# A list schedule in which an exponential of a two-head tile waits for both heads' row maxima

## The chip, the core and the metric

The kernel runs on one core of one Trainium2 chip. A core has five engines with an instruction queue each, which are worked off in order: PE (matmuls; its weight loads are shown as PEld), DVE, ACT, POOL and SP, which here issues the DMAs. The metric is the device time of one execution in microseconds. Times quoted as "the profile's" are from one profiled execution, counted from its first instruction.

## What is computed

One transformer layer with post-normalisation, in float32, over 2 sequences of 1024 tokens of 512 features: causal attention with 16 heads of 32 features, then a feed-forward part whose weights are reduced to their signs.

```python
qkv = x @ w_qkv.T + b_qkv                       # 1536 columns: q, k, v of 16 heads of 32
scores = q @ k.T / sqrt(32) + causal mask       # 1024 x 1024 for each head and sequence
attn = softmax(scores) @ v
x = layernorm(x + attn @ w_out.T + b_out)
hidden = relu((x @ sign(up).T) * up_scale)      # 2048 columns
y = (hidden @ sign(down).T) * down_scale * output_scale
return layernorm(x + y)
```

## The kernel before

**A planner orders everything.** The kernel doesn't write its instructions out in the order in which they run. It describes tasks: which engines can do each (a copy out of PSUM may go to DVE or ACT), what it reads and writes, how long it keeps the engine and when its result is there, and a `place`, which is its priority. `Plan.schedule()` is a list scheduler over these: it steps through a modelled time, gives each free engine the ripe task with the smallest place, and has each buffer class hand out its buffers in the order of places. The order found is recorded under `tc.manual_schedule()`, and each engine's queue follows it. The semaphore waits between engines are put in afterwards, from what the recorded instructions read and write; they are not the planner's. So an edge that the planner does not know changes only the order: the chip still waits as its semaphores say.

**Attention** runs over 8 chunks (2 sequences by 4 groups of four heads). In each chunk come 8 query tiles of 128 rows, i = 0 to 7; tile i sees (i+1)x128 keys. `grouped` says how many heads share one buffer of scores: four for i = 0 and 1, two for i = 2 and 3, one from i = 4 on. In the first chunk it is two heads for i = 0 to 3. So there are 36 tiles of two heads (the profile has 36 L902 on 128x2), with 72 of the 256 exponentials. The last chunk takes its tiles in the order 0, 1, 2, 7, 6, 5, 4, 3.

A tile of scores goes through these steps; the numbers are lines of the kernel:
- L837 on PE writes the scores into one of two PSUM buffers `d` (class "sc", two banks each); L818 does so in the first half of the first chunk, from 32-row operands.
- With one or two heads, L875 on DVE adds the mask and takes the negated row maximum, one instruction per head. With four heads L857 and L867 do it for all four at once.
- L890 on ACT takes the exponential of each head, with that maximum as bias, and sums the rows. When the last one is done the buffer `d` is free for the scores of the next tile but one.
- L902 on DVE takes the reciprocals of the sums, and L908 on POOL multiplies by them.
- L929 on PE transposes the probabilities, 128x128 at a time, four into one PSUM bank `s`; L491 (ACT) or L493 (DVE) copies each bank out.
- L958 on PE multiplies by the values, for all heads of a query tile, and L978 on DVE stores the result in `atT`.

**What fills PE between these steps** is the projection of the next chunk: L553 (keys and queries; their results leave by L632 and L637, or L574, L615 and L620) and L590 (values). In the last chunk it is the output of the second sequence (L1023 on PE; L1017 on POOL adds the bias to the row block `rows`, which has one buffer and comes by DMA; L1034 on DVE adds both), transposes of the first feed-forward block (L1091, copied out by L1098 on ACT and L1103 on DVE), and signs of the weights (L1117 on ACT, from `raw`, which a DMA of 1 MB fills). The feed-forward part (L1140 up, L1177 down) follows.

The scheduler's dependences of the exponential of head j, in `scores`: it reads parts `sc[1, j]`, which the mask or the maximum of head j writes, and `nm[j]`, the maximum itself. With four heads all parts are written by the one mask and the one maximum. With two heads, head 0's exponential is ripe in the planner as soon as head 0's maximum is done.

Of the kernel before, what the change touches and what calls it, by code (L numbers as in the profile page):

```python
# [276 lines left out]
def kernel(  # L277
# [169 lines left out]
    def of(t):  # L447
        if t.cls in rings:
            return rings[t.cls][0][:, t.slot * P : (t.slot + t.blocks) * P]
        if homes[t.cls][t.slot] is None:  # L450
            reopen(t.cls)
        return homes[t.cls][t.slot]
# [16 lines left out]
    def fp32(n):  # L469
        return {"PE": (n / 600 + 0.009,) * 2}  # L470
# [3 lines left out]
    def dve(us):  # L474
        return {"DVE": (us - 0.09, us)}

    def act(us):
        return {"ACT": (us - 0.09, us)}
# [23 lines left out]
    def new(cls, after=(), blocks=1):  # L502
        t = plan.tile(cls, [y for c in after for y in all_of[c]], blocks)
        all_of[cls].append(t)
        return t

    def dma(place, dst, src, kb, reads=(), writes=(), updates=(), queue=DMA, label="dma", after=()):
        def fn(e):
            engine[e].dma_start(dst(), src())

        return plan.task(
            queue, fn, place, reads, writes, updates, size=kb, label=label, after=after
        )
# [3 lines left out]
    def load_x(b, place, blocks):  # L517
        if b not in inputs:
            inputs[b] = new("xT")
        t = inputs[b]  # L520
        for t0 in blocks:
            for c in range(NC):
                latest["x"] = dma(
                    place,
                    lambda t=t, c=c, t0=t0: of(t)[:, c, t0 : t0 + TB],
                    lambda b=b, c=c, t0=t0: xT[ts(c, P), b * S + t0 : b * S + t0 + TB],
                    256,
                    updates=[t[c, t0]],
                )

    def load_w(b, e, place, parts, queue=DMA, after=()):
        if (b, e) not in weights:
            weights[b, e] = new("w")
        t = weights[b, e]
        for n in parts:
            dma(
                place,
                lambda t=t, n=n: of(t)[:, :, n, :],
                lambda n=n, e=e: w_qkvT[:, n * D + e * P : n * D + (e + 1) * P].rearrange(
                    "(c p) f -> p c f", p=P  # L540
                ),
                256,
                updates=[t[n]],
                queue=queue,
                after=after,
            )
# [19 lines left out]
    def bank(ps):  # L566
        return of(ps).rearrange("p a b -> p (a b)")
# [128 lines left out]
    def hold(src, parts, dst, held):  # L696

        for d, h in zip(dst, held):
            plan.task(
                dve(0.15), lambda _, d=d: nc.vector.tensor_copy(d(), src()), -200, parts, [h],  # L700
                label="hold",
            )

    def first_half():

        warm, busy = new("f"), a_x1[:, :P]
        nc.vector.memset(busy, 1.0)
        for k in range(WARM):
            plan.task(
                {"PE": (0.3, 0.3)},  # L710
                lambda _, k=k: nc.tensor.matmul(
                    of(warm)[:, k % 4, :], lhsT=busy, rhs=busy, start=True, stop=True
                ), -300, updates=[warm[0]], label="warm",
            )
        act_queue = {"ACT": (0.5, 0.5)}
        w, biases = new("w"), new("bqk")
        weights[0, 0] = w
        for c, z, n in ((0, 1, 1), (0, 1, 0), (1, NC, 1), (1, NC, 0)):
            dma(
                -100,  # L720
                lambda c=c, z=z, n=n: of(w)[:, c:z, n, :],
                lambda c=c, z=z, n=n: w_qkvT[c * P : z * P, n * D : n * D + P].rearrange(
                    "(c p) f -> p c f", p=P
                ),
                64 * (z - c),
                writes=[w[n, k] for k in range(c, z)],
                queue=act_queue,
            )
            if n == 0 and c == 0:
                dma(-100, lambda: bqk, lambda: b_qkvP, 8, writes=[biases[0]], queue=act_queue)  # L730
        xt = inputs[0] = new("xT")
        for c in range(NC):
            dma(
                -100,
                lambda c=c: of(xt)[:, c, :TB],
                lambda c=c: xT[ts(c, P), :TB],
                256,
                updates=[xt[c, 0]],
            )
        hold(  # L740
            lambda: of(xt)[:, 0, 0:1], [xt[0, 0]],
            [lambda: of(w)[:, 0, 2, 0:1], *[lambda c=c: of(xt)[:, c, TB : TB + 1] for c in range(NC)]],
            [w[2], *[xt[c, TB] for c in range(NC)]],
        )
        load_w(0, 0, -90, [2])
        load_x(0, -80, [TB])
        v, kq = new("v"), new("pt", blocks=8)
        rows = lambda n: of(kq)[:, n * TB : (n + 1) * TB]
        both = {n: new("f") for n in (1, 0)}
        for c in range(NC):  # L750
            for n in (1, 0):
                plan.task(
                    fp32(TB),
                    lambda _, c=c, n=n: nc.tensor.matmul(  # L754
                        bank(both[n]),
                        lhsT=of(w)[:, c, n, :],
                        rhs=of(xt)[:, c, :TB],
                        start=(c == 0),
                        stop=(c == NC - 1),
                    ),  # L760
                    -50, [xt[c, 0], w[n, c]], updates=[both[n][0]], count=2,
                    label="ps",
                )
        for n in (1, 0):
            bias = bqk[:, n * NC : n * NC + 1]
            if n == 0:
                plan.task(
                    dve(0.74),
                    lambda _, bias=bias: nc.vector.tensor_scalar(
                        rows(0), bank(both[0]), bias, scale, ALU.add, ALU.mult  # L770
                    ),
                    -50, [both[0][0], biases[0]], [kq[0]], label="bias",
                )
            else:
                plan.task(
                    act(0.69),
                    lambda _, bias=bias: nc.scalar.activation(
                        rows(1), bank(both[1]), AF.Identity, bias=bias
                    ),
                    -50, [both[1][0], biases[0]], [kq[1]], label="bias",  # L780
                )
        values_of(0, 0, v, 0, lambda units=0: -1)
        plain[0, 0] = kq, v
# [25 lines left out]
    def scores(b, e, i, heads, at):  # L809
        G, N, W = len(heads), (i + 1) * P, 2 * TB // len(heads)  # L810
        sc, nm, sums = new("sc"), new("nm"), new("sums")
        pr = new("pr", blocks=G * (i + 1))
        if (b, e) in plain and i < NQ // 2:
            kq = plain[b, e][0]

            def fn(_):
# [11 lines left out]
                updates=[sc[0]], count=2 * G, label="sc4",  # L828
            )
        else:  # L830
            st = made[b, e][0]
            for j, u in enumerate(heads):
                for k0 in range(0, N, TB):
                    k1 = min(k0 + TB, N)

                    def fn(_, j=j, u=u, k0=k0, k1=k1):
# [11 lines left out]
                        updates=[sc[0]], label="sc",  # L848
# [21 lines left out]
        else:  # L870
            for j in range(G):
# [3 lines left out]
                    lambda _, j=j, some=some: nc.vector.tensor_tensor_reduce(  # L875
                        some(),
                        some(),
                        mask[:, S - N :],
                        scale=-1.0,
                        scalar=LARGEST,  # L880
                        op0=ALU.add,
                        op1=ALU.min,
                        accum_out=of(nm)[:, j : j + 1],
# [3 lines left out]
        for j in range(G):  # L887
            plan.task(
                {"ACT": (0.25 + 0.852 * N / 1000, 0.37 + 0.852 * N / 1000)},
                lambda _, j=j: nc.scalar.activation(  # L890
                    of(pr)[:, j * N : (j + 1) * N],
                    of(sc)[:, j * W : j * W + N],
                    AF.Exp,
                    bias=of(nm)[:, j : j + 1],
                    scale=sign,
                    accum_out=of(sums)[:, j : j + 1],
                ),
                at, [sc[1, j], nm[j]], [pr[j], sums[0]], label="exp",
            )
        plan.task(  # L900
            dve(0.16),
# [3 lines left out]
        for j in range(G):  # L905
            plan.task(
                pool(0.254 + 0.843 * N / 1000),
                lambda _, j=j: nc.gpsimd.tensor_scalar(  # L908
                    of(pr)[:, j * N : (j + 1) * N],
                    of(pr)[:, j * N : (j + 1) * N],  # L910
                    of(sums)[:, j : j + 1],
                    1.0,
                    ALU.mult,
                    ALU.mult,
                ),
# [324 lines left out]


    first_half()
    second_half()
    for at, (b, e) in enumerate(chunks):
# [114 lines left out]
```

## Time and profile before

| what | value |
|---|---|
| time, median of 3 runs | 768.37 us (768.11 to 768.95) |
| the profiled execution | 768.15 us |
| its span, first to last instruction | 766.4 us |
| granted PE clock | 0.998 |
| PE busy | 753.0 us, 98% |
| DVE, ACT, POOL busy | 487.5, 374.9, 258.5 us |
| chain that ended last | PE 90%, DVE 6%, ACT 2%, DMA 1% |

"Busy" is the union of an engine's instruction records. A row of the timeline reads: start, length, engine, line, operation, output and input by name, shapes, count, and in brackets how long the engine was idle ahead of it and whose result ended that. A row of a windows answer gives the window, its length, and the busy time of each engine with its number of instructions. In all rows L numbers are lines of the kernel. DVE writes the maximum itself with a short extra record (DVE_READ_ACCUMULATOR2, 0.14 us), and ACT its row sum with another (ACTIVATION_READ_ACCUMULATOR, 0.2 us).

### The profile page before, as it was taken

To read this page: it belongs to the slowest core of one execution; us is meant where nothing else is said; L and a number is where in the kernel's file an instruction comes from. 1 tells how busy PE (TensorE), PEld (TensorE's weight loads), DVE (VectorE), ACT (ScalarE), POOL (GpSimd) and SP (SyncE) were. 2 spreads that over 40 slices of the span, in tenths; PEclk is the share of its full clock that TensorE was granted. 3 is DMA by queue.
4 is the path that set the end of the run, shared out by engine and by line. 5 is a ranking of instruction groups with operands and counts; after the bars stand their busy time and mean duration, and the time that the engine had idled before them with its cause. 6 is when DMAs were issued, how large, how long until landed. Compare 5 with 4: busy or idle time off the path is not lost.

```text
span 766.4 us, 15395 instructions
## 1 busy us (share of the span) xinstructions
PE 753.0 (98%) x5858; PEld 571.3 (75%) x5858; DVE 487.5 (64%) x1165; ACT 374.9 (49%) x831; POOL 258.5 (34%) x328
## 2 busy tenths in 40 slices
PE   9999999999999999999999999999999999999995
PEld 5668768769756766886876986658777887778884
DVE  2657777777856678877877778855336337335525
ACT  2458666765834465676676587733223222222210
POOL 2426445445525453544544545531002002002000
PEclk9999999999999999999999999999999999999999
DMA  6577345156354225514505523333001001000101
GB/s 189 125 161 152 106 99 125 41 111 170 107 125 102 65 69 110 110 46 91 132 1 113 124 75 122 137 110 110 0 1 56 0 1 56 0 1 1 55 1 55
DMA packets 38216, 62.35 MB, mean 81 GB/s; under 512 B 6144, under 2 KB 18432, under 8 KB 38144
## 3 DMA queue, kind: packets, MB, share of 16 engines
q1 hardware_dynamic: 36912, 60.85, 31.1%
q8 instruction: 46, 0.75, 0.4%
q10 hardware_dynamic: 1232, 0.53, 0.3%
q14 instruction: 26, 0.21, 0.1%
HBM read 24.66 MB, written 4.19 MB: 38 GB/s over the span
## 4 chain that ended last, share of the span: by engine, by line
PE 90%; DVE 6%; ACT 2%; DMA 1%; issue 1%; POOL 0%; ACTq 0%
PE s L929 15%; PE s L1140 14%; PE pd L1177 14%; PE s L553 12%; PE d L837 9%; PE s L958 8%; PE s L590 8%; PE s L1023 7%; DVE d L875 2%; ACT probs L890 1%; PE s L754 1%; PE s L1091 1%; DVE small L1207 1%; DMA rows<-in_x 1%; PE d L818 1%
## 5 line engine op out<-in xcount | busy, mean ns | idle before, releaser
L908 POOL TENSOR_SCALAR probs<-probs,small 128x128 f32<-128x128 f32 (+7 forms) x256 | 188.5, 747 | 235.7 <-DVE small L902 194.0
L890 ACT ACTIVATE probs<-d,small 128x128 f32<-128x128 f32 (+7 forms) x256 | 189.9, 750 | 50.8 <-DVE small L875 25.3
L875 DVE CUSTOM_DVE_ANT_0 d<-d,mask 128x384 f32<-128x384 f32 (+7 forms) x200 | 173.7, 876 | 25.3 <-PE d L837 20.2
L929 PE MATMUL s<-ident,probs 128*128 128x128 f32 x1152 | 160.1, 273 | 0.8 <-DVE small L902 0.4
L491 ACT COPY probsT<-s 128x512 f32<-128x512 f32 (+3 forms) x193 | 98.4, 542 | 127.1 <-PE s L929 113.3
L929 PEld LDWEIGHTS s<-ident,probs 128*128 128x128 f32 x1152 | 133.3, 141 | 32.2 <-issue 23.2
L1177 PE MATMUL pd<-stacks,hid 128*128 128x512 f32 x512 | 133.0, 399 | 0.5 <-DVE hid L1157 0.5
L1140 PE MATMUL s<-xt,stacks 128*128 128x512 f32 x512 | 132.7, 399 | 0.0
L1151 ACT ACTIVATE hf<-s,ups 128x512 f32<-128x512 f32 x64 | 44.1, 690 | 164.3 <-PE s L1140 162.5
L553 PE MATMUL s<-xT,wqkv 128*128 128x512 f32 x240 | 119.2, 597 | 0.0
L837 PE MATMUL d<-stacks 128*128 128x512 f32 (+2 forms) x368 | 114.0, 409 | 2.8 <-ACT probs L890 2.8
L1177 PEld LDWEIGHTS pd<-stacks,hid 128*128 128x128 f32 x512 | 94.1, 188 | 24.2 <-DVE hid L1157 1.4
L1140 PEld LDWEIGHTS s<-xt,stacks 128*128 128x128 f32 x512 | 94.2, 188 | 23.4 <-issue 1.0
L1157 DVE CAST hid<-hf 128x512 fp32r<-128x512 f32 x64 | 27.3, 427 | 121.6 <-ACT hf L1151 121.5
L493 DVE COPY probsT<-s 128x512 f32<-128x512 f32 (+3 forms) x152 | 83.7, 561 | 24.7 <-PE s L929 22.5
L837 PEld LDWEIGHTS d<-stacks 128*128 128x128 f32 x368 | 58.2, 189 | 38.5 <-ACT probs L890 19.6
L590 PE MATMUL s<-wqkv,xT 128*128 128x128 f32 x512 | 75.9, 275 | 0.0
L590 PEld LDWEIGHTS s<-wqkv,xT 128*128 128x128 f32 x512 | 68.6, 191 | 8.8 <-issue 7.3
L958 PEld LDWEIGHTS s<-probsT,v 128*32 128x32 f32 x2304 | 60.3, 110 | 19.3 <-ACT probs L890 7.6
L958 PE MATMUL s<-probsT,v 128*32 128x128 f32 x2304 | 71.7, 274 | 0.0
L1023 PE MATMUL s<-wout,atT 128*128 128x512 f32 x128 | 63.5, 596 | 0.4 <-ACT probsT L491 0.4
L890 ACT ACTIVATION_READ_ACCUMULATOR probs<-d,small 128x1 f32 x256 | 53.2, 208 | 0.0
(68 smaller groups left out, 492.4 us busy)
## 6 DMA issues: line engine op xcount, KB each, us to landing
stacks<-wqkv SPq DMA_DIRECT2D x224, 128.0 KB, 2.4
wqkv<-in_w_qkvT SPq DMA_DIRECT2D x22, 256.0 KB, 3.3
xT<-in_xT SPq DMA_DIRECT2D x16, 256.0 KB, 4.7
rows<-in_x SPq DMA_DIRECT2D x16, 256.0 KB, 2.8
raw<-in_up_wT SPq DMA_DIRECT2D x4, 1024.0 KB, 5.0
out<-atT SPq DMA_DIRECT2D x16, 256.0 KB, 2.0
stacks<-wqkv SPq DMA_DIRECT2D x48, 64.0 KB, 2.0
raw<-in_down_wT SPq DMA_DIRECT2D x2, 1024.0 KB, 5.4
```

The lines of the kernel that those rows point to most:

```text
L491: nc.scalar.copy(dst, src)
L553: nc.tensor.matmul(of(ps).rearrange("p a b -> p (a b)"), lhsT=of(w)[:, c, n, :], rhs=of(xt)[:, c, t0 : t0 + TB], start=(c == 0), stop=(c = ...
L590: nc.tensor.matmul(of(ps)[:, t, :], lhsT=of(xt)[:, c, t0 + t * P : t0 + (t + 1) * P], rhs=of(w)[:, c, 2, :], start=(c == 0), stop=(c == NC ...
L837: nc.tensor.matmul(of(sc)[:, j * W + k0 : j * W + k1], lhsT=of(st)[:, 0, u, ts(i, P)], rhs=of(st)[:, 1, u, k0:k1], start=True, stop=True,)
L875: lambda _, j=j, some=some: nc.vector.tensor_tensor_reduce(some(), some(), mask[:, S - N :], scale=-1.0, scalar=LARGEST, op0=ALU.add, op1= ...
L890: lambda _, j=j: nc.scalar.activation(of(pr)[:, j * N : (j + 1) * N], of(sc)[:, j * W : j * W + N], AF.Exp, bias=of(nm)[:, j : j + 1], sca ...
L908: lambda _, j=j: nc.gpsimd.tensor_scalar(of(pr)[:, j * N : (j + 1) * N], of(pr)[:, j * N : (j + 1) * N], of(sums)[:, j : j + 1], 1.0, ALU. ...
L929: lambda _, k=k, c=c, tp=tp: nc.tensor.transpose(of(tp)[:, k, :], of(pr)[:, c], ident),
L958: nc.tensor.matmul(of(to)[ts(u, HD), n, :], lhsT=of(v)[:, k, ts(u, HD)], rhs=of(pt)[:, ts(c + k, P)], start=(k == i), stop=(k == 0),)
L1023: lambda _, c=c: nc.tensor.matmul(bank(py), lhsT=of(a)[:, c, :], rhs=of(wout)[:, c, :], start=(c == 0), stop=(c == NC - 1),),
L1140: lambda _, f=f, c=c, n=n, pu=pu: nc.tensor.matmul(of(pu), lhsT=of(up)[:, f // TPB, c, ts(f % TPB, P)], rhs=of(xt)[:, n, c, :], start=(c = ...
L1177: lambda _, f=f, t=t, n=n, h=h: nc.tensor.matmul(of(pds[t]), lhsT=of(h)[:, ts(t, P)], rhs=of(dn)[:, f // 4, f % 4, :], start=(f == 0 and n ...
```

## The change

Two places change. In the planner's task of the exponential, the one part `sc[1, j]` that it reads becomes the parts of all heads of the tile. For tiles of one head or of four heads this adds nothing to what it waited for; for tiles of two heads, both heads' exponentials are ripe only when both maxima are done. The warm-up matmuls get `count=2`, a field that other tasks have too. No instruction is added or removed by either edit; `Plan.schedule()` is run on the changed tasks, and all engines' orders come out of it anew.

```diff
@@ -710,7 +710,7 @@ first_half
                 {"PE": (0.3, 0.3)},
                 lambda _, k=k: nc.tensor.matmul(
                     of(warm)[:, k % 4, :], lhsT=busy, rhs=busy, start=True, stop=True
-                ), -300, updates=[warm[0]], label="warm",
+                ), -300, updates=[warm[0]], count=2, label="warm",
             )
@@ -895,7 +895,7 @@ scores
                     scale=sign,
                     accum_out=of(sums)[:, j : j + 1],
                 ),
-                at, [sc[1, j], nm[j]], [pr[j], sums[0]], label="exp",
+                at, [*[sc[1, k] for k in range(G)], nm[j]], [pr[j], sums[0]], label="exp",
             )
```

## The prediction

> **What bounds the kernel now.** I read the page first, then who waited for whom on PE, then windows around the places that this list points to, then the timeline there. The page says that PE is the bound:
>
> ```profile
> span 766.4 us, 15395 instructions
> PE 753.0 (98%) x5858; PEld 571.3 (75%) x5858; DVE 487.5 (64%) x1165; ACT 374.9 (49%) x831; POOL 258.5 (34%) x328
> ```
>
> PE lacks 13.4 us of the span. By the chain of waits 1.0 us of that lies ahead of the first matmul and 7.8 behind the last (it ends at 758.6). The rest, 4.6 us, is stalls, and the list of waits and the windows tell where:
>
> ```profile
> PE d L837 <- ACT probs L890: 2.8, 8, 0.9
> PE s L1023 <- ACT probsT L491: 0.4, 1, 0.4
> ```
> ```profile
> 91.50:115.00 23.50, 22.57 (x175) 14.86 (x174) 17.80 (x51) 15.13 (x36) 10.42 (x14) 1.00 0.37 82
> 148.00:171.00 23.00, 22.43 (x174) 14.74 (x174) 16.78 (x49) 15.24 (x36) 10.43 (x14) 1.00 0.41 91
> 453.00:506.00 53.00, 51.79 (x472) 35.36 (x474) 43.78 (x109) 38.29 (x69) 25.50 (x27) 1.00 0.37 125
> 513.00:758.00 245.00, 244.51 (x1075) 195.27 (x1074) 113.59 (x224) 59.71 (x92) 16.79 (x12) 1.00 0.06 23
> ```
>
> Columns: window; its length, busy time of PE, PEld, DVE, ACT, POOL; clock, DMA. PE lacks 0.93, 0.57 (the same again at 342-365 and 398-421) and 1.21 us; in 245 us of feed-forward only 0.49. The timeline shows what such a stall is:
>
> ```profile
> 149.15 0.70 DVE L875 CUSTOM_DVE_ANT_0 d<-d,mask 128x512 f32<-128x512 f32 x1 [0.62 <-PE d L837]
> 149.94 0.70 DVE L875 CUSTOM_DVE_ANT_0 d<-d,mask 128x512 f32<-128x512 f32 x1
> 150.79 0.69 ACT L890 ACTIVATE probs<-d,small 128x512 f32<-128x512 f32 x1 [1.12 <-DVE small L902]
> 150.88 1.02 PE L553 MATMUL s<-xT,wqkv 128*128 128x512 f32 x2
> 151.47 0.68 ACT L890 ACTIVATE probs<-d,small 128x512 f32<-128x512 f32 x1
> 152.29 0.56 PE L837 MATMUL d<-stacks 128*128 128x512 f32 x2 [0.38 <-ACT probs L890]
> ```
>
> This is a tile of two heads. Its first maximum ends at 149.85, its second at 150.64; ACT is idle, yet the first head's exponential starts at 150.79, behind the second maximum. So the chip already waits for both, and the planner did not know it: it put the scores of the next tile but one (same buffer) too early on PE, at 152.29, where they wait for the second exponential (ends 152.15, plus 0.14 of handing over).
>
> The records understate it: an L553 is recorded at 0.59 but passes every 0.43. I call that its turn (L837 of 512 columns 0.23, L929 0.11, L590 0.11). Counted from turns this stall is 152.29 less (151.32+0.43), 0.54; the one at 148.38 is 0.35, the one at 94.72 is 1.10.
>
> **The change, part by part.** The orders of the two built programs can be laid side by side; they hold the same matmuls, maxima, exponentials and DMAs.
>
> *count=2 on the warm-up matmuls.* A task keeps this field and the scheduler never reads it: 0.
>
> *Where the order moves.* The edit adds no wait on the chip. PE's order differs in seven stretches, in before's time A 16.5-28, B 91.5-115, C 148-171, D 198-210, E 342-365, F 398-421, G 453-506; C, E and F are one order, three times, before and after. Outside them PE is unchanged, feed-forward included. 21 copies from PSUM go from DVE to ACT: on ACT 11 and 12 more of 512 and 128 columns, 2 fewer of 256. By the rows this is 11x0.59+12x0.27-2x0.38 = 9.0 us on ACT for 10.1 off DVE (0.69, 0.28, 0.41 each). Neither is the bound, so it counts only through who stands ahead of whom.
>
> *C, walked (E and F alike).* I name a tile by query tile and heads: 3/01 and 3/23 have two heads, 4/0 to 4/3 one. 2/23's two exponentials now stand behind three copies, where before they had two copies between them: they end at 148.24, as before (148.23). PE does the values of tiles 0 and 1 (24 rows, 0.70) ahead of 3/23's scores, from 148.04 to 148.83; these then find their buffer free (148.24+0.14): the stall of 0.35 is gone. They take 0.47 and a 0.07 break, so 3/23's maxima start at 149.6 and 150.4, its exponentials at 151.25 and, behind a bias (L632, 0.7), 152.5; the buffer is free at 153.3. PE meanwhile does 4/0's scores (0.29), twelve transposes (1.31) and three L553 pairs (2.58), two pairs and six transposes more than before, and comes to 4/1's scores at 153.5: the stall of 0.54 is gone, with 0.2 to spare. Next, 4/1's scores and seven transposes (1.05) bring 4/2's to 154.6; 4/0's exponential, behind 3/23's last (ends 153.2) and a copy of 2/23, runs to 154.35, so the buffer is free at 154.5; 5/0's at 157.1, free at 157.0; 5/3's, 6/0's and 6/1's have 0.15, 0.4 and 0.05 to spare. These margins are smaller than my errors, so of 0.90 I leave 0.15 behind: 0.75 for each of C, E, F; bounds 0.3 (two margins missed by 0.3) and 0.9. Sum 2.25.
>
> *A reciprocal between two maxima.* In B, C, E and F the tile ahead's L902 comes to stand between 3/23's maxima. Before has this too, at 24.31 and 25.14: 0.83 from start to start, against 0.79 without it (149.15 to 149.94). So 0.04, within the margins: 0. By the Trainium skill, "VectorE: DVE Perf Modes", section "The DRAIN you can't avoid", a DVE instruction starts only once the one in front is flushed, with semaphores or without. By that rule it would cost its own 0.16, four times 0.12 more, and the sum would give 765.0; the trace's 0.04 does not agree.
>
> *B.* Stalls of 1.10 and 0.13 (at 100.20), same cause. After's order is C's from 4/0 on, so the same margins: 1.0; bounds 0.4 and 1.2.
>
> *A.* Here scores are L818, of 32 rows, two heads a tile, and alternate with two L553 or six L590. Starts on the timeline give the loss: 20.37 to 21.42 is 1.05 for two L553 (0.86); 22.27 to 23.13 and 24.19 to 25.08 are 0.86 and 0.89 for six L590 (0.67): 0.19, 0.19, 0.22 lost. After, score tiles stand in pairs with twenty L590 between: one such break for three. 0.4; bounds 0.1 and 0.6.
>
> *D.* No stall now. After, 3/23's scores move ahead of an L553 pair and meet 2/23's exponentials (free at 202.8, PE there at 202.55): a loss of 0.2; bounds 0.4 and 0.
>
> *G.* The end of attention: the last outputs with their one rows buffer, the first block's turn, signs of the up weights. Stalls by turns: 0.25 in 453-456, 0.97 in 486-489, 1.45 in 497-501, 2.67 in all.
>
> ```profile
> 486.21 0.30 PE L929 MATMUL s<-ident,probs 128*128 128x128 f32 x1 [0.20 <-POOL rows L1017]
> 488.24 1.12 PE L1023 MATMUL s<-wout,atT 128*128 128x512 f32 x2 [0.45 <-ACT probsT L491]
> 497.38 1.74 PE L929 MATMUL s<-ident,probs 128*128 128x128 f32 x10 [0.37 <-DVE small L902]
> ```
>
> After, the last two-head scores stand 1.6 us earlier on PE, which helps the 1.45. But tile 5's values come up 0.65 us behind the transposes that they need, and their two copies stand on ACT behind a sign (1.92): 0.6 to 1.6 lost. And L1017, which waits for rows (4.6 to 5.7 us from issue to landing beside a weight load), stands on POOL ahead of the last two normalisations, whose transposes are due then: some 0.7. Net 0.4 gained; bounds a loss of 1.0 and a gain of 2.0. The last rows load moves behind two down-weight loads on SP; what it feeds is turned for the third block, 100 us later: 0.
>
> Sum: 0.4+1.0+2.25-0.2+0.4 = 3.85. The profiled execution took 768.15 us, 1.75 of it around the span; it would take 764.3. From the median, 768.37, that is 764.5.
>
> **Rivals.** *G recovers nearly all*, 2.0 instead of 0.4: 762.9. For it: DVE is the busiest engine behind PE there (43.8 of 53 us) and is relieved. Against: the sign in the way.
>
> *The stalls come back*: B, C, E, F gain nothing, since margins of 0.05 to 0.2 miss by 0.3 each; 768.4-0.6 = 767.8, or 766.1 if half comes back. For it: five tight margins in each stretch. Against: a stall gives its time to the next margin, so they do not add.
>
> *Slower: copies ahead of exponentials on ACT.* In these four stretches the exponentials of 5/1, 5/2 and 5/3 come to stand behind copies that wait for PE's own transposes (of 4/0, 4/1, 4/2). If they end later than PE's arrival at the scores that reuse the buffer, less 0.14, PE waits for the exponential, and the exponential for a copy and PE: up to a copy's 0.59 each, 1.77 a stretch. Against 0.90 saved (1.23 in B) this is 3x0.87+0.54-0.6 = 2.55 more: 770.9. It decides from 0.05 to 0.4 us of lateness on, by my walk.
>
> *It does not do what it says*: the stalls stay, since the chip waited for both maxima already: 768.4. Against: at each stalled place PE's order is changed.
>
> **Numbers.** Forecast 0.60 (764.5, its own range 762.8 to 766.6), G recovers 0.18, stalls come back 0.12, slower 0.06, nothing 0.04. About 0.2%, 1.5 us, can be told from no change, so faster is below 766.8. Faster: 0.59 of the forecast, 0.18, and 0.05 of the returning stalls: 0.82. Slower 0.06, same 0.12. All best bounds together are 6.5 us, 761.9; behind a stall two score matmuls also stand 0.1 further apart (152.29, 152.63), up to 0.6 more: the low end is 761.3. The high end, 767.9, takes in the returning stalls and leaves out the slower case, the unchanged one and some of the tails.
>
> **What would show it.** Right: L837 waits for L890 under 1 us in all instead of 2.8, PE busy within 0.2 us of the length in C, E and F, PE's busy time the same within 1 us, the feed-forward starting 3 to 5 us earlier at the same length. Wrong: L837 still waits for L890 at 4/2, 5/3 or 6/1, in three equal stretches (the margins), or G is longer than 53 us (the sign, L1017).

## The result, and the profile after

The changed kernel takes 762.88 us (median of 4 runs, 762.47 to 763.08) against 768.66 us for the kernel before, run beside it (4 runs, 768.11 to 769.8). The ratio is 0.9922, with a 95% interval of 0.9905 to 0.9939: about 5.8 us less. The profiled execution took 762.84 us, with a span of 761.0.

I read the page first, then the list of what PE waited for.

```profile
span 761.0 us, 15415 instructions
PE 749.5 (98%) x5858; PEld 572.0 (75%) x5858; DVE 481.6 (63%) x1144; ACT 381.4 (50%) x852; POOL 258.0 (34%) x328
```
```profile
PE s L929 <- DVE probsT L493: 1.0, 2, 0.5
PE s L929 <- ACT probsT L491: 0.5, 1, 0.5
...
PE s L553 <- DMA wqkv<-in_w_qkvT: 0.4, 1, 0.4
PE d L837 <- ACT probs L890: 0.2, 1, 0.2
```

The columns of the second fence are the total, the number of times and the longest wait. The line to find is the last: scores that wait for exponentials, 2.8 us in 8 places before, are one place of 0.2 us. Seven of the 8 lay in B, C, E and F and are gone; the one that is left, at 309.23, is the eighth (311.70 before), and the last section comes back to it. New are three waits for copies of transposed tiles (L491, L493; all in G) and one for a weight load. The windows show B, C, G and a stretch of feed-forward, each moved to where it lies after. PE is full in B and C, as it is in E (339 to 361) and F (394 to 416); in G it is not.

```profile
90.50:113.50 23.00, 23.00 (x177) 15.20 (x176) 16.95 (x46) 17.50 (x43) 9.73 (x13) 1.00 0.42 93
145.60:167.50 21.90, 21.90 (x173) 14.31 (x171) 15.44 (x44) 16.76 (x41) 9.43 (x13) 1.00 0.42 91
447.50:499.90 52.40, 50.82 (x481) 35.60 (x482) 43.32 (x108) 39.15 (x72) 24.07 (x26) 1.00 0.38 127
507.60:752.60 245.00, 244.49 (x1074) 195.29 (x1073) 115.69 (x227) 59.60 (x92) 16.59 (x12) 1.00 0.06 23
```

In C the timeline shows that the chip does the same as before, and that only PE's place in it moved:

```profile
148.29 0.70 DVE L875 CUSTOM_DVE_ANT_0 d<-d,mask 128x512 f32<-128x512 f32 x1
148.90 0.16 DVE L902 RECIPROCAL small<-small 128x2 f32<-128x2 f32 x1
149.08 0.70 DVE L875 CUSTOM_DVE_ANT_0 d<-d,mask 128x512 f32<-128x512 f32 x1
...
149.93 0.69 ACT L890 ACTIVATE probs<-d,small 128x512 f32<-128x512 f32 x1 [0.27 <-POOL probs L908]
...
151.18 0.69 ACT L890 ACTIVATE probs<-d,small 128x512 f32<-128x512 f32 x1
...
151.41 1.02 PE L553 MATMUL s<-xT,wqkv 128*128 128x512 f32 x2
152.01 0.46 PEld L837 LDWEIGHTS d<-stacks 128*128 128x128 f32 x2 [0.40 <-ACT probs L890]
152.01 0.72 PE L837 MATMUL d<-stacks 128*128 128x512 f32 x2
```

Tile 3/23's first exponential still starts at 149.93, 0.15 after the second maximum's end (149.08 and 0.70); the chip's wait is there as before. (The bracket names POOL's L908, whose two records from 147.35 had ended at 148.49; the maximum came later.) The second exponential ends at 151.87, and 0.14 later 4/1's scores, which reuse the buffer, are let go: their weight load carries the bracket. But PE's own row has none. PE now has two L553 pairs and six transposes more in front, the last pair from 151.41; by two turns of 0.43 it is at work until 152.27, so the buffer is free 0.26 us before PE needs it. (The 0.72 of these two scores, instead of the usual 0.54, is their record lying over the pair's.)

To find where the time went I counted PE's work in turns and noted, in each trace, when the same amount of it had been done. The table gives the change of that lead against before, stretch by stretch (negative is time saved), for the kernels of the experiments too. "Start" is up to 14 us, where PE waits for the first loads; these land up to 1.9 us earlier or later from one execution to the next, so that row, and the sum with it, is not the kernel's alone. "D to E" is 222 to 338 us. G's row runs to the end. The stretches left out are within 0.1 us but for one: in edge_in_cef, scores at 136 us lose 0.75 us to a late stack transfer.

| stretch | after | edge_in_cef | copies_as_before | copies_as_after | one_head_tiles | weights_earlier | priced_longer |
|---|---|---|---|---|---|---|---|
| start | +0.36 | +1.11 | +1.86 | +0.01 | +0.64 | +0.75 | +1.26 |
| A | -0.97 | -0.01 | -0.96 | -0.02 | -0.01 | -0.96 | -0.15 |
| A to B | +0.64 | +0.01 | +0.74 | +0.05 | +0.23 | +0.11 | +0.25 |
| B | -1.42 | +0.02 | -1.10 | -0.90 | -1.69 | -1.35 | -1.41 |
| C | -1.12 | -1.11 | -1.04 | +0.11 | -1.19 | -0.97 | -0.82 |
| D | -0.08 | -0.01 | -0.19 | +1.15 | -0.16 | -0.06 | -0.12 |
| D to E | +0.11 | -0.61 | -0.61 | -0.61 | -0.72 | -0.60 | -0.58 |
| E | -1.12 | -1.13 | -1.05 | +0.09 | -1.22 | -1.12 | -0.81 |
| F | -1.13 | -1.12 | -1.06 | +0.08 | -1.20 | -1.12 | -0.83 |
| G and on | -0.63 | +0.07 | -0.58 | -0.52 | -0.82 | -0.61 | +0.19 |

### The profile page after: what moved, and what is told of

Read it like the earlier page. It is cut to its first block, busy times and chain, and to the rows that moved or that the text cites. A ratio compares the mean times of both kernels' runs of the same rounds, so it can differ in the third digit from the quotient of the medians.

```text
span 761.0 us, 15415 instructions
## 1 busy us (share of the span) xinstructions
PE 749.5 (98%) x5858; PEld 572.0 (75%) x5858; DVE 481.6 (63%) x1144; ACT 381.4 (50%) x852; POOL 258.0 (34%) x328
## 4 chain that ended last, share of the span: by engine, by line
PE 92%; DVE 5%; ACT 1%; SPq 1%; DMA 0%; issue 0%; ACTq 0%
PE s L929 16%; PE s L1140 15%; PE pd L1177 15%; PE s L553 13%; PE d L837 9%; PE s L958 9%; PE s L1023 7%; PE s L590 7%; PE s L754 1%; SPq L509 1%; DVE small L1207 1%; PE s L1091 1%; DVE atT L1191 1%; DVE d L875 1%; DVE x L1066 1%; PE s L711 1%
## 5 line engine op out<-in xcount | busy, mean ns | idle before, releaser
L908 POOL TENSOR_SCALAR probs<-probs,small 128x128 f32<-128x128 f32 (+7 forms) x256 | 188.5, 747 | 234.0 <-DVE small L902 178.7
L890 ACT ACTIVATE probs<-d,small 128x128 f32<-128x128 f32 (+7 forms) x256 | 189.9, 751 | 35.3 <-DVE small L875 15.9
L491 ACT COPY probsT<-s 128x512 f32<-128x512 f32 (+3 forms) x214 | 105.7, 530 | 129.7 <-PE s L929 115.1
L929 PE MATMUL s<-ident,probs 128*128 128x128 f32 x1152 | 162.4, 273 | 1.6 <-DVE probsT L493 1.0
L929 PEld LDWEIGHTS s<-ident,probs 128*128 128x128 f32 x1152 | 133.9, 141 | 32.6 <-issue 22.3
L553 PE MATMUL s<-xT,wqkv 128*128 128x512 f32 x240 | 118.1, 595 | 0.4 <-DMA wqkv<-in_w_qkvT 0.4
L837 PE MATMUL d<-stacks 128*128 128x512 f32 (+2 forms) x368 | 114.2, 408 | 0.2 <-ACT probs L890 0.2
L493 DVE COPY probsT<-s 128x512 f32<-128x512 f32 (+3 forms) x131 | 73.8, 575 | 24.4 <-PE s L929 22.1
L837 PEld LDWEIGHTS d<-stacks 128*128 128x128 f32 x368 | 58.3, 190 | 30.5 <-issue 18.4
L553 PEld LDWEIGHTS s<-xT,wqkv 128*128 128x128 f32 x240 | 39.5, 190 | 21.0 <-issue 19.6
```

The lines of the kernel that those rows point to most:

```text
L491: nc.scalar.copy(dst, src)
L553: nc.tensor.matmul(of(ps).rearrange("p a b -> p (a b)"), lhsT=of(w)[:, c, n, :], rhs=of(xt)[:, c, t0 : t0 + TB], start=(c == 0), stop=(c = ...
L837: nc.tensor.matmul(of(sc)[:, j * W + k0 : j * W + k1], lhsT=of(st)[:, 0, u, ts(i, P)], rhs=of(st)[:, 1, u, k0:k1], start=True, stop=True,)
L890: lambda _, j=j: nc.scalar.activation(of(pr)[:, j * N : (j + 1) * N], of(sc)[:, j * W : j * W + N], AF.Exp, bias=of(nm)[:, j : j + 1], sca ...
L908: lambda _, j=j: nc.gpsimd.tensor_scalar(of(pr)[:, j * N : (j + 1) * N], of(pr)[:, j * N : (j + 1) * N], of(sums)[:, j : j + 1], 1.0, ALU. ...
L929: lambda _, k=k, c=c, tp=tp: nc.tensor.transpose(of(tp)[:, k, :], of(pr)[:, c], ident),
```

## The experiments

My theory: the gain is the stalls at two-head tiles, place by place, and they go because the planner now believes the buffer busy for as long as it is. Rivals: DVE gains from the 21 copies that moved to ACT; or any new layout would have done it. In the kernels named copies_as, three lines were put in front, so there an L number is 3 higher.

**The edge in three head groups only.**

```diff
-                at, [sc[1, j], nm[j]], [pr[j], sums[0]], label="exp",
+                at, [*[sc[1, k] for k in range(G) if k == j or chunks.index((b, e)) in (2, 5, 6)], nm[j]], ...
```

> The edge only in the third, sixth and seventh head group: PE's order is the changed kernel's in stretches C, E and F and the old one everywhere else; 15 of the 21 copies move to ACT. Theory (the gain is the stalls of the two-head tiles, place by place): C, E and F give 1.1 us each as they did in the changed kernel, nothing elsewhere: 3.3 less, about 765.3, and PE's waits at L837 for L890 fall from 2.8 to about 1.1 (B, A and G keep theirs). Rival (the stretches carry over into each other, or the gain is one whole-kernel effect such as a different start): another amount than 3.3, with differences outside C, E and F.

Measured: 765.02 us, against 768.89 for the kernel before beside it; ratio 0.9957 (0.9943 to 0.9972), so 3.3 us less by the ratio and 3.9 by the medians. C, E and F save 1.11, 1.13 and 1.12 us, as in the changed kernel; A, B and G nothing. (The 0.61 between D and E is no gain of the edge: see the last section.) The trace keeps B's stall and has C, E, F full (C's window; then the timeline at B):

```profile
148.80:170.80 22.00, 22.00 (x173) 14.35 (x172) 15.56 (x44) 16.85 (x41) 9.45 (x13) 1.00 0.42 91
```
```profile
95.83 0.56 PE L837 MATMUL d<-stacks 128*128 128x512 f32 x2 [0.92 <-ACT probs L890]
```

So C, E and F are each worth 1.1 us, whether or not A, B and G are changed.

**Which engine copies: two kernels.** The planner chooses the engine of each copy that DVE or ACT may do; here the list ON gives it, a letter for each. One kernel has the edge and before's engines, the other has no edge and after's engines.

```diff
+    either = [t for t in plan.tasks if len(t.engines) == 2 and "ACT" in t.engines and "DVE" in t.engines]
+    for t, e in zip(either, ON):
+        e = "ACT" if e == "A" else "DVE"
+        t.engines = {e: t.engines[e]}
     order = plan.schedule()
```

> The edge everywhere, but each of the copies out of PSUM is bound to the engine that it had before (197 on ACT, 294 on DVE): DVE gets no relief. The planner ends the kernel 0.14 us later than the changed kernel's plan. Theory (the stalls went because the planner now counts the second maximum): nearly the whole gain stays, 763 to 764, L837's wait for L890 under 1 us. Rival (it is the 21 copies, 10 us of work, taken off DVE): no gain, 768 to 769, with the waits of before.

> No edge, but each copy is bound to the engine that it has in the changed kernel (218 on ACT): DVE has the whole relief, the planner still thinks that the first exponential starts behind the first maximum. The plan ends 0.58 us later than before's. Theory: the stalls stay or become other ones of the same kind, L837 waits for L890 2 to 4 us in all, 767.5 to 770. Rival (relief of DVE): 762.5 to 764.

Measured: with the edge and before's engines 762.89 us, ratio 0.9931 (0.9914 to 0.9948). Without the edge and with after's engines 768.44 us, ratio 1.0 (0.999 to 1.001). DVE's busy time is 487.6 us in the first and 479.0 in the second: the kernel whose DVE does the most is the fast one. In the second the stalls of C stand at the same scores as before, at 147.49 (0.17) and 152.16 (waits, then the timeline at the latter):

```profile
PE d L840 <- ACT probs L893: 2.2, 8, 0.4
```
```profile
152.16 0.56 PE L840 MATMUL d<-stacks 128*128 128x512 f32 x2 [0.33 <-ACT probs L893]
```

What B gained there (0.90) went in D (1.15). The relief of DVE is ruled out as the cause of the whole gain, and a new layout alone does not bring it: this one, without the edge, leaves C, E and F as they were. For G it is otherwise: here G saves 0.52 us without the edge, and 0.63 in the changed kernel, so G's gain is not shown to come from the edge.

**One-head tiles for 2 and 3.** Outside the first half of the first chunk, where the edge would act in A, no tile of two heads is left.

```diff
-        g = min(most, 4 if i < 2 else 2 if i < 4 else 1)
+        g = min(most, 4 if i < 2 else 2 if i < 4 and most == 2 else 1)
```

> No edge, and outside the first half of the first head group no tile of two heads: tiles 2 and 3 take one head each, so no maximum shares its buffer with another and the planner's old rule is true there. The number of matmuls, maxima and exponentials is the same, small reciprocals are more. The plan ends 0.15 us later than before's. The span of before was 10.0 us longer than its plan, that of the changed kernel 4.6. Theory (the missing 5.4 are what the planner did not know of two-head tiles): the span comes out 4 to 6 us longer than the plan, so 762 to 764.5 in time, without any edge. Rival (copies on ACT: here 201, nearly as before): 768 to 769. A third: one-head tiles free their buffers differently and cost something of their own, over 765 with waits at L837 that are not for the second maximum.

Measured: 762.66 us, ratio 0.9921 (0.9906 to 0.9936), with no edge at all. In B, C, E and F it saves what the edge saves and 0.07 to 0.27 more. L837's wait for L890 is not in the list; the longest one within the attention is now in G:

```profile
PE s L929 <- POOL rows L1017: 0.6, 1, 0.6
```

Either one tells the planner of the chip's wait, or one makes tiles that do not have it: about 6 us less either way.

**The weights behind A.**

```diff
-        stack(st, 1, hl, TB, TB, TB, lambda: -20)
+        stack(st, 1, hl, TB, TB, TB, lambda: -16)
...
-        stack(st, 0, qh, TB, 0, TB, lambda: -20)
+        stack(st, 0, qh, TB, 0, TB, lambda: -16)
...
-            load_w(nb, ne, base - 15, [1, 0, 2], after=[] if at else [latest["x"]])
+            for parts, place in (([1], -18), ([0, 2], base - 15)) if not at else (([1, 0, 2], base - 15),):
+                load_w(nb, ne, place, parts, after=[] if at else [latest["x"]])
```

> The changed kernel, with the key weights of the second head group sent off on SP between the first and the second 16 stack transfers, instead of behind the first 32; the two other weight parts stay. In the changed kernel's trace A saves 0.97 us and 0.65 of it goes at 36.09, where L553 waits 0.52 for these weights. Theory (A's gain is given back to this transfer, which is simply sent too late for a PE that comes earlier): no stall at L553 near 36 us, 0.4 to 0.6 less than the changed kernel, about 762.4. Rival (the transfer's landing in that one run): nothing changes in the median; or a stack transfer, now 0.6 later, is waited for instead. PE's order behind 49 us is laid out a little differently, up to 0.3 either way.

Measured: 761.95 us, ratio 0.9915 (0.9902 to 0.9929). Against the changed kernel's 0.9922 the intervals overlap, so the timeline has to decide. First the changed kernel, then this one:

```profile
36.09 1.10 PE L553 MATMUL s<-xT,wqkv 128*128 128x512 f32 x2 [0.35 <-DMA wqkv<-in_w_qkvT]
```
```profile
35.10 1.88 PE L553 MATMUL s<-xT,wqkv 128*128 128x512 f32 x4
```

The L553 runs on without a bracket, and of A's 0.96 only 0.11 is given back up to B. In the changed kernel it was 0.64, of which the wait at 36.09 is 0.52 by turns. (The planner, told of the earlier weights, also puts this L553 ahead of six transposes.) That the transfer was late by chance in one execution is ruled out by copies_as_before, which has the same order here and waits at the same L553, at 37.67, for 0.42. A's gain was real; a transfer that used to arrive just in time took about half of it.

**A longer price instead of the edge.**

```diff
-                {"ACT": (0.25 + 0.852 * N / 1000, 0.37 + 0.852 * N / 1000)},
+                {"ACT": (0.25 + 0.852 * N / 1000 + 0.4 * (G == 2), 0.37 + 0.852 * N / 1000 + 0.4 * (G == 2))},
```

> No edge; the planner is told instead that each exponential of a two-head tile takes 0.4 us longer, so that it believes the tile's buffer free 0.8 us later, about as late as it really is. The plan ends 0.73 us later than before's. Theory (what matters is when the planner believes the buffer free, not that it is told the reason): most of the waits of L837 for L890 go, 2.8 to under 1.2 us, 764 to 766. Rival (the order needs the true dependence, since the price also makes ACT look busier than it is and moves other work): gain under 1.5 us, over 767.

Measured: 765.12 us, ratio 0.9957 (0.9944 to 0.9969), in the theory's range. The waits of L837 for L890 are gone from the list. But C, E and F save 0.82, 0.81 and 0.83 instead of 1.12, and A and G next to nothing: a wrong reason that gives the right date helps where that date matters and lays out the rest for an ACT that does not exist.

**Towards a faster kernel.** One-head tiles, the edge (it then acts in A alone) and the earlier weights together; then also each sign cut in two:

```diff
-        plan.task(
-            act(1.9), lambda _: nc.scalar.activation(of(t)[:, g], of(raw), AF.Sign), on,
-            [raw[0]], [t[g]], label="sign",
-        )
+        for k in (0, 1):
+            plan.task(
+                act(1.05),
+                lambda _, k=k: nc.scalar.activation(
+                    of(t)[:, g, 2 * k : 2 * k + 2], of(raw)[:, 2 * k : 2 * k + 2], AF.Sign
+                ), on, [raw[0]], [t[g]], label="sign",
+            )
```

> Three things together: one-head tiles for 2 and 3, the edge (it then acts only in the first half of the first head group, stretch A), the key weights earlier. If A's 0.97 is kept and nothing of it is given back, 0.9 less than the one-head kernel (762.66): 761.5 to 762.0. If the weights or a stack are still waited for: 762.3 or more.

> As the kernel ahead, and each of the eight signs, 1.93 us on ACT, is cut in two halves of about 1.0, so that a copy or an exponential waits at most half as long behind one. The plan ends 1.93 us earlier. Theory (in G the signs stand ahead of copies that PE waits for, as the prediction had it): G's stalls, 1.7 us in the one-head kernel, fall by half or more, 760.0 to 761.0. Rival (G's stalls are rows on POOL and turns on DVE, not the signs): within 0.4 of the kernel ahead.

Measured: 761.54 us, ratio 0.9912 (0.9898 to 0.9926), and 759.35 us, ratio 0.9882 (0.9866 to 0.9897). The second is the fastest version here; its interval ends below where the changed kernel's begins. In its G PE waits for nothing:

```profile
446.00:498.00 52.00, 52.00 (x449) 36.04 (x447) 44.44 (x116) 39.46 (x78) 26.06 (x28) 1.00 0.36 112
```

That looked like proof that the signs had been in the way. Three more kernels were run to see: the halves in the changed kernel alone; the one-head kernel with whole signs and a price of 2.0 instead of 1.9, which only lays G out anew; and the order of the fastest kernel with each sign whole, in the place of its second half.

```diff
-            act(1.9), lambda _: nc.scalar.activation(of(t)[:, g], of(raw), AF.Sign), on,
+            act(2.0), lambda _: nc.scalar.activation(of(t)[:, g], of(raw), AF.Sign), on,
```
```diff
-                lambda _, k=k: nc.scalar.activation(
-                    of(t)[:, g, 2 * k : 2 * k + 2], of(raw)[:, 2 * k : 2 * k + 2], AF.Sign
+                lambda _, k=k: k and nc.scalar.activation(
+                    of(t)[:, g], of(raw), AF.Sign
                 ), on, [raw[0]], [t[g]], label="sign",
```

> The changed kernel with each sign cut in two halves, nothing else (two-head tiles and weights as changed). In its G four stalls (0.25, 0.68, 0.71, 0.60) follow a sign of 1.93 us on ACT. The plan ends 0.53 us later than the changed kernel's, and puts the two halves of the fourth sign back to back. Theory (a sign's length ahead of copies is what G loses by, as the prediction had it): G's stalls fall from 2.2 to under 1.2 us, 761.3 to 762.2. Rival (the gain seen with one-head tiles was the order that the planner happened to lay out there, since halves back to back block as long as a whole): 762.5 to 763.8, with stalls of 1.8 us or more in G.

> The kernel of one-head tiles, edge and earlier weights with whole signs, of which the planner is told 2.0 us instead of 1.9 (on the chip 1.93): no work is changed, only G is laid out anew. Its plan ends 0.65 us later. Theory (the halves made the 2.0 us gain): G keeps about its 1.7 us of stalls, 761 to 762.5. Rival (any other layout of G can gain or lose that much, since G has six kinds of work with tight dates): a change of 0.8 us or more either way.

> The order of the one-head kernel with halved signs (759.35), instruction for instruction, but each sign is executed whole, 1.93 us, in the place of its second half; the place of the first half is left empty. Theory (the order that the planner laid out, not the halves, saved G's 2.0 us): 759.0 to 760.0, no stall over 0.3 us in G. Rival (the shorter block on ACT saved it): G's stalls are back, 1 to 2 us of them, 760.5 to 761.5.

Measured: 763.23 us (ratio 0.9924, 0.9912 to 0.9937), 761.76 us (0.9908, 0.9894 to 0.9921) and 759.97 us (0.9886, 0.9869 to 0.9902). In the first the halves run back to back (ACT's row, two records; the sign is L1119 where it is cut). PE's three brackets in G come to 1.9 us by turns (0.44 at 483.33, then 0.82 and 0.60), where the changed kernel's four stalls come to 2.2. But 25 transposes from 470.63 on take 3.5 us, where turns give 2.7, in small losses without a bracket, and G saves 0.21 us instead of 0.63 (PE's rows):

```profile
481.72 2.02 ACT L1119 ACTIVATE stacks<-raw 128x1024 fp32r<-128x1024 f32 x2
```
```profile
470.63 3.50 PE L929 MATMUL s<-ident,probs 128*128 128x128 f32 x25
...
484.83 0.63 PE L929 MATMUL s<-ident,probs 128*128 128x128 f32 x4 [0.66 <-DVE probsT L493]
```

In the third, a whole sign runs on ACT from 481.39 to 483.34, and PE is full around it; in the same window of the changed kernel, which has a sign at 481.50, PE lacks 1.58 us (ACT's timeline; the window):

```profile
481.39 1.95 ACT L1119 ACTIVATE stacks<-raw 128x2048 fp32r<-128x2048 f32 x1
```
```profile
478.00:497.00 19.00, 19.00 (x142) 13.07 (x141) 17.12 (x50) 15.30 (x33) 9.50 (x11) 1.00 0.32 105
```

In G and behind it, the three kernels of one-head tiles and earlier weights save 0.81 us (signs whole), 2.96 (halved) and 2.50 (whole, in the halved order). So of the 2.15 between the first two, 1.69 is the order and 0.46 the shorter sign. The 0.46 has a place: in the third kernel PE waits for an exponential that stands on ACT right behind a whole sign, 0.40 by turns, and the kernel with halves has no wait there (ACT's row, then PE's):

```profile
462.03 1.92 ACT L1119 ACTIVATE stacks<-raw 128x2048 fp32r<-128x2048 f32 x1
...
464.99 0.50 PE L837 MATMUL d<-stacks 128*128 128x512 f32 x1 [0.23 <-ACT probs L890]
```

The last kernel's time was as its theory expected; that no stall over 0.3 us would be left in G was not. The kernel with the sign priced otherwise came out as the other side expected (761 to 762.5; G saves 0.35): not every new layout brings the gain. So a sign's length does cost PE time, but most of what the halves seemed to bring was the order. This is shown for the one-head kernel; the changed kernel with whole signs in a better order was not run.

## Why the prediction was right, point by point

**What bounds the kernel, and the mechanism.** Right, and shown three ways: the stalls go with the edge, they stay without it, and they go when tiles 2 and 3 have one head each. The edit `count=2` was not run alone; in the kernel a task only keeps the field, and nothing reads it. The stalls did not come back, and no exponential behind a copy became late for PE: L837's one remaining wait for L890 is the 0.2 us of the last section.

**C, E, F.** Forecast 0.75 each, measured 1.12. The term was mis-sized in both of its parts. None of the margins that I called smaller than my errors was missed, so the 0.15 left behind each time was not; and behind a stall the stalled pair of scores also stands further apart, which I had kept for the low end of the range only. The stalls were 0.90 by turns, so 0.22 of the 1.12 is that.

**A reciprocal between two maxima.** I took 0. In the fence of C above the maxima start 0.79 us apart (148.29 and 149.08) with the reciprocal between them, exactly as without it before. The 0.16 that follows from the Trainium skill, "VectorE: DVE Perf Modes", section "The DRAIN you can't avoid", is not seen here either. The prediction gave that rule too widely: the same section adds that a next instruction that is not held starts earlier.

**B.** Forecast 1.0, measured 1.42 (1.23 of stalls and the same extra); bounds 0.4 and 1.2 were too narrow at the top.

**A.** Forecast 0.4, bounds 0.1 and 0.6; measured 0.97, then 0.64 lost up to B, most of it to the weight load: net 0.33 saved. So the net came near the forecast by luck: two terms were missing, and they nearly cancel. The first is in the scores themselves, which I had left as they were. Before, two sets of four L818 of 384 columns take 0.85 us each (19.52 to 20.37, 21.42 to 22.27); after, all eight in a row take 1.16 (20.72 to 21.88), 0.54 less (the second row of before, then after):

```profile
21.42 0.91 PE L818 MATMUL d<-probsT 32*128 32x384 f32 x4
```
```profile
20.72 1.23 PE L818 MATMUL d<-probsT 32*128 32x384 f32 x8
```

Why eight in a row pass faster was not tried; the eight of 512 columns do not. For the second, my step asked what is late next for the exponentials' readers, but not what is late next for a PE that arrives early. The weights were issued on SP behind 32 stack transfers both times; before, PE came to them at 36.09 anyway.

**D.** Forecast a loss of 0.2, measured a saving of 0.08.

**G.** Forecast 0.4, measured 0.63, with the reason only half right. That the edge is the cause is not shown, since a layout without it saved 0.52 (copies_as_after). A loss stands where I put it: L929 waits for copies at 483.33 and 484.73, beside a sign from 481.50 to 483.43.

```profile
481.50 1.93 ACT L1117 ACTIVATE stacks<-raw 128x2048 fp32r<-128x2048 f32 x1
...
483.33 0.85 PE L929 MATMUL s<-ident,probs 128*128 128x128 f32 x6 [0.51 <-DVE probsT L493]
484.73 0.52 PE L929 MATMUL s<-ident,probs 128*128 128x128 f32 x3 [0.55 <-ACT probsT L491]
```

By turns these two are 0.68 and 0.71, 1.39 in all, inside my 0.6 to 1.6. But in the one-head kernel a whole sign at about that time cost nothing in another order, so the sign's length is not shown to be the reason here. A third stall, 0.60 by turns at 494.43, is where I had expected 0.7 from L1017; PE's bracket there names a copy (L493), so what L1017 cost stays open.

**What was to be seen.** L837's wait is 0.2 us (under 1 was asked). PE is full in B, C, E and F to the hundredth. The feed-forward has the same length (244.49 busy of 245.00, before 244.51) and lies 5.4 us earlier, a little beyond the 3 to 5. One sign failed: PE's busy time fell by 3.5 us, where I had it the same within 1. A record of a matmul ahead of a stall is longer than its turn, so of the 5.4 us only 1.9, net, had been shown as idle; I had written that the records understate a stall and did not apply it to this line.

**The sum.** 3.85 forecast, 5.4 found in the span. The surplus is 1.1 in C, E and F, 0.4 in B, 0.3 in D and 0.2 in G; A's net was 0.1 short, and 0.5 was lost at the start and between D and E, where the change has no part. The median came out at 762.88, at the lower edge of my own range for the forecast, because B, C, D, E and F ended beyond their better bounds. So the mechanism was right, and the sizes of B, C, E and F were too small. The rival that G recovers nearly all gives the same time, 762.9, but for a wrong reason: G saved 0.63, not 2.0.

## What to carry to other kernels

Where a planner orders the work, compare when the chip starts an instruction with what the planner waits for: a dependence that the chip enforces and the plan lacks can put other engines' work too early, here in four of eight chunks, and it can be mended by telling the plan or by shaping the tile so that the dependence is gone. Ask of each gain what PE reaches next, transfers included, and price such a gain at the whole stall by turns, not at the idle time in the records. Before a stall is put down to a long instruction beside it, run the same order with that instruction unchanged, since a new layout alone moved a stretch here by 1.7 us.

## What the runs showed of the hardware

Between D and E, where PE's order was left alone, before and after lose 0.6 to 0.8 us on PE that the table's other kernels do not lose, and of those not in the table edge_half_signs alone loses it too; 0.36 of it is the stall at 309.23, the 0.2 us wait of L837 for L890. It goes with one L1066 (normalisation on DVE, from SBUF to SBUF) that meets an L908 on POOL. The groups' rows give shortest, median and longest in ns; the first is after, the second the kernel with earlier weights, and POOL's rows follow in the same order:

```profile
L1066 DVE TENSOR_SCALAR x<-x,small x8: 537/540/1140, 300.3 to 304.7; 128x512 f32<-128x512 f32 x8
```
```profile
L1066 DVE TENSOR_SCALAR x<-x,small x8: 537/541/545, 300.2 to 304.6; 128x512 f32<-128x512 f32 x8
```
```profile
304.30 1.25 POOL L908 TENSOR_SCALAR probs<-probs,small 128x768 f32<-128x768 f32 x1 [4.36 <-DVE small L902]
```
```profile
304.21 1.63 POOL L908 TENSOR_SCALAR probs<-probs,small 128x768 f32<-128x768 f32 x1 [4.35 <-DVE small L902]
```

With two-head tiles it goes one of two ways. In before, after and edge_half_signs DVE's last L1066 takes 1.14 us instead of 0.54, POOL's L908 takes 1.25, and the chain behind DVE reaches PE. In the other five POOL's takes 1.63 instead of 0.91, DVE's keeps its 0.54, and PE feels nothing. (With one-head tiles the longest L1066 is 0.63 to 0.74.) The Trainium skill, "SBUF — State Buffer", section "Who interferes with whom", says that DVE in its two-port modes, which a `tensor_scalar` can enter, shares a port pair with GpSimd, that whoever issues first keeps it for the whole instruction, and that issue order decides who blocks. The trace agrees that one of the two waits, but its starts do not tell which: in all eight kernels L908 starts 0.07 us behind one L1066 and 0.38 ahead of the last. No run here tried to keep the two apart.
